# A Mamba stage in one kernel: diagonals of B through DRAM, root of token sums on GpSimd, states kept by VectorE, edges in one sum, and the pieces of a body at other slots

## The chip, the cores and the metric

The kernel runs on one core of a Trainium2 chip. A core has five engines with instruction streams of their own, each worked off in order: TensorE (PE; its weight loads are shown apart as PEld), VectorE (DVE), ScalarE (ACT), GpSimd (POOL) and SyncE (SP), which here only issues DMA transfers. They meet through semaphores. The metric is the time of one execution on the device in microseconds (us), the median of the runs; lower is better.

## The reference, cut to what matters

The whole model is a MetaFormer block: a convolution and attention layer, a recurrence over 4096 tokens (normalise, one matrix, a sigmoid), eight Mamba layers, and a mixture of experts. The change lies in the Mamba layers. For every layer, with L = 4096 tokens, four batch elements, 128 model channels, 256 inner channels d and 16 states s:

```python
xz = x @ Wi
xi, z = jnp.split(xz, 2, axis=-1)
xp = jnp.pad(xi, ((0, 0), (D_CONV - 1, 0), (0, 0)))
xc = sum((xp[:, k:k + L, :] * cw[:, k] for k in range(D_CONV))) + cb
xc = jax.nn.silu(xc)
dbl = xc @ Wx                       # 8 columns for dt, 16 for B, 16 for C
dt = jax.nn.softplus(dt_r @ Wdt + bdt)
dA = jnp.exp(dt[..., None] * A)
dBx = (dt * xc)[..., None] * Bs[:, :, None, :]
h = scan(dA, dBx)                   # h[t] = dA[t] * h[t-1] + dBx[t]
y = jnp.einsum('blds,bls->bld', h, Cs) + Dp * xc
y = y * jax.nn.silu(z)
out = rmsnorm(y @ Wo)               # x * rsqrt(mean(x * x) + eps) * w
```

## The kernel before, in words

The sequence is cut into 8 chunks of TL = 512 tokens. A *body* is one chunk of one layer of one batch element: 8 x 8 x 4 = 256 bodies, in the order chunk, layer, batch element. Channels lie on the 128 partitions, so the 256 inner channels are two halves (h = 0, 1) and tokens run along the free dimension. All data are float32.

A body has NSLOT = 16 slots. A slot is one pair of states of one half of the channels: slots 0 to 7 are half 0 with pairs 0 to 7, slots 8 to 15 half 1 with pairs 7 down to 0. In a slot j of body o the loop at the end of `mamba` issues, in this order, on whatever engine each belongs to:

- `decay` for two slots ahead: ScalarE's exponentials dA (L976), two of 128x512;
- `inputs` for one slot ahead: TensorE makes dBx, the product of dt times x with B (L998). B is a value per token, so it is brought in as a diagonal matrix: the tokens of dt times x lie on partitions (`dtxT`), and eight 64-row products with `diag` give 512 tokens x 2 states in PSUM. `diag` is built by VectorE (`diag`, L964): the transposed B (`bt`, in PSUM) times an identity, one 128x512 product per pair of states, seven a body. The last pair (slots 7 and 8) goes another way: GpSimd multiplies (`times_b`, by0 and by1, L1019), and dA lies in PSUM (dAp);
- `scan`: VectorE's two scans (L1031), hs = dA * state + dBx;
- `times_c` at every odd slot, for a group g of four states: GpSimd copies the last column of hs into `state` (L1044), and then multiplies 128x2048 values by the broadcast C (L1047), which a DMA has brought into `Cb` out of the scratch `c_d`;
- `side`, the pieces of the string `PLAN`, in two parts; between them `add_up`, TensorE's transposes that add the groups' products into yT (L1051), four slots late.

The pieces carry the rest of the body: for the next body (n) the projection (`v`), the short convolution (`tap`, VectorE; the first three tokens of a chunk need the last three of the chunk before, which `edge` computes on GpSimd, L832 to L839, and six 128x1 activations bring in, L854), silu, the gate's projection (`pz`), `pd` (dt, B and C in small), `pt` (dt in full), softplus, `dtx` (GpSimd, L937) and `turn`; for the body itself `leave`, `back`, `gate`; for the body before (q) the output projection `po` and the normalisation: `square`, `pm` (the mean over channels by a product with a matrix of 1/128, L1101), Ln and Exp on ScalarE (`log`, `rstd`), and u = pos * r on GpSimd (`u`, L1112). Where a chunk begins, the pieces s and z do a layer normalisation of the input (`mean`, `var`, `lnv`, `rstd`, `u`). Each row of `PLAN` is a slot; the letter names the body.

PSUM has two banks f0 and f1 for all pieces (`BANK` says which), four for dBx and dAp (two buffers of two), one for yT. Buffers come free when their last reader is done, and an instruction that needs one waits in its engine's stream with everything behind it. The recurrence of the layer before runs on underneath: `rec.step`, a product of 128x4 (L669) and a tanh (L672), as often in a slot as `STEPS` says; its first 576 steps run alone, and in the last 36 bodies there are none left.

ScalarE must load a table of functions where two neighbouring functions lie in different sets (ACT_TABLE_LOAD); the pieces `exp` and `ln` do that by hand.

Of the kernel before, what the change touches and what calls it, by code (L numbers as in the profile page):

```python
# [610 lines left out]
class Recurrence:  # L611
# [44 lines left out]
    def step(self, t):  # L656

        nc = self.nc
        n, k = divmod(t, RT)
        if k == 0:  # L660

            self.wx, self.x1 = self.got.pop(n)
            self.p = self.ps.tile([P, RT, B], F32, tag="p", name="p")
            nc.tensor.matmul(
                self.p, self.ops.ident, self.wx.rearrange("p b t -> p t b"), start=True, stop=False,
                skip_group_check=True,
            )
            self.z = self.w.tile([P, RT, B], F32, tag="z", name="z")
        nc.tensor.matmul(  # L669
            self.p[:, k, :], self.vt, self.before, start=False, stop=True, skip_group_check=True  # L670
        )
        nc.scalar.activation(self.z[:, k, :], self.p[:, k, :], AF.Tanh, scale=0.5)  # L672
        self.before = self.z[:, k, :]
        if k == RT // 2 and n + 1 < L // RT:
            self.load(n + 1)
        if k == RT - 1:
            y = self.w.tile([P, RT, B], F32, tag="y", name="y")
            nc.gpsimd.tensor_scalar(y, self.z, 0.5, 0.5, ALU.mult, ALU.add)
            nc.gpsimd.tensor_tensor(self.x1, self.x1, y.rearrange("p t b -> p b t"), ALU.add)
            here = (slice(None), slice(None), slice(n * RT, (n + 1) * RT))  # L680
            nc.sync.dma_start(out=self.x2_d[here], in_=self.x1)
# [11 lines left out]
s.mean n.v0 |  # L693
s.var |
| n.tap03 n.tap02 o.C3
n.v1 | q.leave1 o.by0
n.tap01 | o.by1 q.back1
q.gate1 |
| n.tap12 q.po0 n.tap13 n.tap11
q.po1 | q.square n.pz0 n.pz1 n.silu n.silu_z0 n.silu_z1 a.exp  # L700
n.pd0 | n.pd1 z.fetch n.keep
n.pt0 n.C2 n.pt1 | n.softplus0 q.pm n.softplus1 a.ln q.log q.rstd s.lnv s.rstd a.exp
n.dtx0 n.bt n.B |
q.u | s.u o.leave0 n.diag0
n.turn0 n.skip0 n.skip1 | n.diag2
o.back0 n.diag5 | q.end n.diag3
n.diag1 n.C0 o.gate0 n.dtx1 | n.C1
n.diag4 n.turn1 n.diag6 m.edge |
""".strip().split("\n")
STEPS = [1, 0, 1, 2, 1, 1, 1, 0, 1, 0, 1, 0, 2, 2, 2, 1]  # L710

BANK = {
    "v0": 0, "v1": 1, "pz0": 0, "pz1": 1, "pd": 0, "pt0": 1, "pt1": 0, "bt": 0, "turn0": 1,
    "turn1": 1, "back0": 1, "back1": 0, "po": 0, "pm": 1, "mean": 1, "var": 1,
# [12 lines left out]
def mamba(tc, ops, I, rec, x2_d, x3_d):  # L727
# [13 lines left out]
    SP_B = SP - 1  # L741
    with ExitStack() as ctx:
        dap = ctx.enter_context(tc.tile_pool(name="mda", bufs=4))
# [24 lines left out]
        i64 = c.tile([P, 64], F32, name="i64")  # L768
        nc.vector.tensor_tensor(i64, ops.ident[:, 0:64], ops.ident[:, 64:P], ALU.add)
# [10 lines left out]

        us = {}
        weights = {}
# [25 lines left out]
        def mean(o):  # L808
            m = bank("mean")
            nc.tensor.matmul(m, ops.avg, o.x2, start=True, stop=True)  # L810
            o.pos = w1.tile([P, TL], F32, tag="xm", name="xm")
            nc.vector.tensor_tensor(o.pos, o.x2, m, ALU.subtract)
            nc.scalar.activation(o.x2, o.pos, AF.Square)

        def var(o):
            o.r = w1.tile([P, TL], F32, tag="r0", name="r0")
            v = bank("var")
            nc.tensor.matmul(v, ops.avg, o.x2, start=True, stop=True)
            nc.scalar.copy(o.r, v)

        def log_var(o):
            nc.scalar.activation(o.r, o.r, AF.Ln, bias=ops.eps6)


        def edge(o):

            o.edge = w.tile([P, NH, DC - 1], F32, tag="edge", name="edge")
            part = w.tile([P, NH, DC - 1, DC - 1], F32, tag="part", name="part")
            for h in range(NH):
                tl = tail[:, o.l, o.b, h, :]  # L830
                for k in range(DC - 1):
                    nc.gpsimd.tensor_tensor(  # L832
                        part[:, h, k, :],
                        tl[:, k : k + DC - 1],
                        taps[:, o.l, h, k : k + 1].to_broadcast([P, DC - 1]),
                        ALU.mult,
                    )
            nc.gpsimd.tensor_tensor(o.edge, part[:, :, 0, :], part[:, :, 1, :], ALU.add)
            nc.gpsimd.tensor_tensor(o.edge, o.edge, part[:, :, 2, :], ALU.add)  # L839

        def proj(o, h):
# [10 lines left out]
            nc.scalar.activation(o.xc[:, h, n:], v[:, n:], AF.Copy, scale=t)  # L852
            for k in range(n):
                nc.scalar.activation(  # L854
                    o.xc[:, h, k : k + 1], v[:, k : k + 1], AF.Identity, scale=t,
                    bias=o.edge[:, h, k : k + 1],
                )
# [62 lines left out]
        def step_proj(o, h):  # L920
            if h == 0:
                o.pt = {}
            o.pt[h] = bank(f"pt{h}")
            at = W_DT + h * P
            nc.tensor.matmul(
                blocks(o.pt[h]), o.given[:, at : at + P], o.dbl, start=True, stop=True
# [31 lines left out]
        def diag(o, sp):  # L958

            if sp == 0:  # L960
                o.diag = w.tile([P, SP_B, NB, 64, 2], F32, tag="diag", name="diag")
            at = RK + 2 * sp
            bt = o.BT.rearrange("p (n r) -> p n r", n=NB)[:, :, at : at + 2]
            nc.vector.tensor_tensor(  # L964
                o.diag[:, sp],
                bt.unsqueeze(2).to_broadcast([P, NB, 64, 2]),
                i64.unsqueeze(1).unsqueeze(3).to_broadcast([P, NB, 64, 2]),
                ALU.mult,
            )


# [13 lines left out]
        def inputs(o, j):  # L985
# [8 lines left out]
            for n in range(NB):  # L994
                for q in range(2):
# [5 lines left out]
                        o.diag[row, sp, n],  # L1001
# [24 lines left out]
        def scan(o, j):  # L1026
            sp, h = where(j)
            hs = states(o, j)
            for k in range(2):
# [8 lines left out]
                )  # L1038

        def times_c(o, g):  # L1040
# [3 lines left out]
            nc.gpsimd.tensor_copy(  # L1044
                state[:, o.l, o.b, h, 4 * f : 4 * f + 4].unsqueeze(2), hs[:, :, TL - 1 : TL]
            )
# [52 lines left out]
        def rms(o):  # L1099
            o.pm = bank("pm")  # L1100
            nc.tensor.matmul(o.pm, ops.avg, o.sq, start=True, stop=True)  # L1101

        def log(o):
            o.r = w1.tile([P, TL], F32, tag="r", name="r")
            nc.scalar.activation(o.r, o.pm, AF.Ln, bias=ops.eps5)

        def rstd(o):
            nc.scalar.activation(o.r, o.r, AF.Exp, scale=-0.5)

        def norm(o):  # L1110
            o.out = us[o.b] = up.tile([P, TL], F32, tag="u", name="u")
            nc.gpsimd.tensor_tensor(o.out, o.pos, o.r, ALU.mult)  # L1112

        def end(o):
            here = (slice(None), o.b, slice(o.ck * TL, (o.ck + 1) * TL))
            x3 = w1.tile([P, TL], F32, tag="x3", name="x3")
# [13 lines left out]
        def table(name):  # L1130
# [11 lines left out]
        pieces |= {f"diag{k}": lambda o, k=k: diag(o, k) for k in range(SP_B)}  # L1142
# [3 lines left out]
            "fetch": fetch, "mean": mean, "var": var, "lnv": log_var, "silu": silu_x, "keep": keep,  # L1146
            "B": give_b,
            "bt": turn_b, "square": square, "pm": rms, "log": log, "rstd": rstd, "u": norm,
            "end": lambda o: end(o) if o.l == DEPTH - 1 else None, "edge": edge,
            "exp": table(EXP_TANH), "ln": table(EXP_LN),  # L1150
# [10 lines left out]
        for t in range(PRE):  # L1161
            rec.step(t)
        for s in bodies[0:3]:
            for what in ("fetch", "mean", "var", "lnv", "rstd", "u"):
                pieces[what](s)
        fetch(bodies[3])
        edge(bodies[0])
        for row in plan:
            for part in row:
                for k, what in part:  # L1170
                    if k == "n":
                        pieces[what](bodies[0])
        decay(bodies[0], 0)
        decay(bodies[0], 1)
        edge(bodies[1])
        inputs(bodies[0], 0)
        LAG = 4
        t = PRE
        for i in range(len(bodies) + 1):
# [3 lines left out]
            who["s"] = s if s and s.l == 0 else None  # L1183
            who["z"] = z if z and z.l == 0 else None
            if not o:
                who["a"] = None
                nc.scalar.preload_act_table_set(EXP_LN)
            if o and o.b == 1 and i + 3 < len(bodies):
                load((o.l + 1) % DEPTH)
            for j in range(NSLOT):  # L1190
                if o:
                    if j + 2 < NSLOT:
                        decay(o, j + 2)
                    elif n:
                        decay(n, j + 2 - NSLOT)
                    if j + 1 < NSLOT:
                        inputs(o, j + 1)
                    elif n:
                        inputs(n, 0)
                    if STEPS[j] > 0 and t < L:  # L1200
                        rec.step(t)
                        t += 1
                    scan(o, j)
                    if j % 2:
                        times_c(o, j // 2)
                side(who, j, 0)
                if o and j in (LAG, SP + LAG):
# [6 lines left out]
                if o and STEPS[j] > 1 and t < L:  # L1214
                    rec.step(t)
# [367 lines left out]
def layouts(a):  # L1583
# [31 lines left out]
    for h in range(NH):  # L1615
        ch = slice(h * P, (h + 1) * P)
        given[:, :, W_X + h * P : W_X + h * P + RK + 2 * NS] = f["L1_conv_W_xproj"][:, ch]
        given[:, :, W_OUT + h * P : W_OUT + (h + 1) * P] = f["L1_conv_W_out"][:, ch]
    given[:, :RK, W_DT : W_DT + DI] = f["L1_conv_W_dt"]
# [32 lines left out]
```

## Time and profile before

Three runs: median 15734.69 us (15732.74 to 15743.9). The profiled execution's own time is its span.

| | us |
|---|---|
| median of the runs | 15734.69 |
| profiled execution, span | 15742.0 |
| PE busy | 14396.9 (91%) |
| POOL busy | 13176.9 (84%) |
| DVE busy | 13692.5 (87%) |
| ACT busy | 12015.6 (76%) |
| first scan of the Mamba stage begins | 2215.23 |
| its last scans begin | 15448.80 |
| 8000 to 12000: PE, DVE, POOL, ACT busy of 4000 | 3789.45, 3682.95, 3712.28, 3207.24 |

A line of a timeline has the start and the length in us, engine, source line, operation, output<-inputs, and how many instructions it merges; in brackets, how long the engine sat idle before it and what ended that. A group of the page has busy time in all and the mean of one in ns, and after the bar the idle time before its instructions. A line of the waits says who waited for whom, in all, how often and at most. Matrix products overlap, so the distance between starts says more than their lengths.

### The profile page before, as it was taken

To read this page: it belongs to the slowest core of one execution; us is meant where nothing else is said; L and a number is where in the kernel's file an instruction comes from. 1 tells how busy PE (TensorE), PEld (TensorE's weight loads), DVE (VectorE), ACT (ScalarE), POOL (GpSimd) and SP (SyncE) were. 2 spreads that over 40 slices of the span, in tenths; PEclk is the share of its full clock that TensorE was granted. 3 is DMA by queue.
4 is the path that set the end of the run, shared out by engine and by line. 5 is a ranking of instruction groups with operands and counts; after the bars stand their busy time and mean duration, and the time that the engine had idled before them with its cause. 6 is when DMAs were issued, how large, how long until landed. Compare 5 with 4: busy or idle time off the path is not lost.

```text
span 15742.0 us, 303070 instructions
## 1 busy us (share of the span) xinstructions
PE 14396.9 (91%) x120596; PEld 10815.0 (69%) x120596; DVE 13692.5 (87%) x14955; ACT 12015.6 (76%) x23617; POOL 13176.9 (84%) x9086
## 2 busy tenths in 40 slices
PE   6888779999999999999999999999999999999996
PEld 3444557777777777777777777777777777766665
DVE  8998039998999899998999899989998999999994
ACT  6888247887888778877888788878888788777773
POOL 4555039999999999999999999999999999999994
PEclk8999569999999999999999999999999999999998
DMA  0000012222222222222222222222222222222224
GB/s 22 22 22 22 15 50 100 104 98 105 97 97 104 97 106 99 97 107 96 104 98 97 105 97 104 101 102 101 95 103 102 100 104 97 103 97 97 102 93 176
DMA packets 423478, 1431.59 MB, mean 91 GB/s; under 512 B 204080, under 2 KB 204464, under 8 KB 290864
## 3 DMA queue, kind: packets, MB, share of 16 engines
q1 hardware_dynamic: 421920, 1411.95, 24.9%
q8 instruction: 952, 15.60, 0.4%
q14 instruction: 462, 3.78, 0.1%
q10 hardware_dynamic: 144, 0.26, 0.0%
HBM read 1353.33 MB, written 58.72 MB: 90 GB/s over the span
## 4 chain that ended last, share of the span: by engine, by line
POOL 61%; issue 11%; ACT 10%; PE 9%; DVE 7%; DMA 1%; POOLq 0%; SPq 0%; ACTq 0%; DVEq 0%
POOL hs L1047 46%; POOL hs L1019 6%; POOL dtx L937 4%; ACT dA L976 4%; DVE hs L1031 2%; DVE acc L278 2%; POOL state L1044 2%; POOL u L1112 2%; PE yT L1051 2%; POOL part L832 1%; PE f L849 1%; ACT L1131 1%; PE xm L221 1%; PE dBx L998 1%; ACT xc L854 1%
## 5 line engine op out<-in xcount | busy, mean ns | idle before, releaser
L1031 DVE TENSOR_TENSOR_SCAN hs<-dA,state,dBx 128x512 f32<-128x512 f32 x7168 | 8714.0, 1262 | 992.7 <-PE dBx L998 872.1
L1047 POOL TENSOR_TENSOR hs<-hs,Cb 128x2048 f32<-128x2048 f32 x2048 | 9294.6, 4538 | 166.2 <-POOL state L1044 1.5
L976 ACT ACTIVATE dA<-dt,A 128x512 f32<-128x512 f32 x7168 | 4728.6, 722 | 7.4 <-DVE hs L1031 1.2
L1051 PE MATMUL yT<-ident,hs 128*128 128x128 f32 x32768 | 4334.5, 276 | 8.8 <-POOL hs L1047 8.8
L1051 PEld LDWEIGHTS yT<-ident,hs 128*128 128x128 f32 x32768 | 3785.6, 144 | 772.5 <-issue 650.3
L998 PE MATMUL dBx<-diag,dtxT 64*128 64x128 f32 x57344 | 4188.2, 286 | 70.9 <-DVE hs L1031 44.8
L998 PEld LDWEIGHTS dBx<-diag,dtxT 64*128 64x128 f32 x57344 | 3512.3, 188 | 1026.5 <-issue 696.9
L672 ACT ACTIVATE z<-p 128x4 f32<-128x4 f32 x4096 | 711.3, 174 | 1575.4 <-PE p L669 1569.5
L669 PE MATMUL p<-z,vt 128*128 128x4 f32 x8192 | 1579.3, 263 | 238.6 <-ACT z L672 232.4
L669 PEld LDWEIGHTS p<-z,vt 128*128 128x128 f32 x8192 | 1350.3, 207 | 635.1 <-ACT z L672 377.5
L1019 POOL TENSOR_TENSOR hs<-Bb,dtx 128x512 f32<-128x512 f32 x1024 | 1275.0, 1280 | 5.5 <-PE yT L1051 4.5
L1031 DVE TENSOR_TENSOR_SCAN hs<-dAp,state,hs 128x512 f32<-128x512 f32 x1024 | 1228.2, 1261 | 0.0
L863 DVE SCALAR_TENSOR_TENSOR xc<-f,taps,xc 128x509 f32<-128x509 f32 (+2 forms) x1536 | 1129.4, 735 | 42.2 <-ACT tail L858 15.0
L964 DVE TENSOR_TENSOR diag<-f,i 128x512 f32<-128x512 f32 x1792 | 1156.3, 669 | 9.3 <-PE f L952 9.3
L1044 POOL COPY state<-hs 128x4 f32<-128x4 f32 x2048 | 388.0, 189 | 779.9 <-DVE hs L1031 621.5
L1131 ACT ACT_TABLE_LOAD x768 | 985.3, 1283 | 10.4
L278 DVE SCALAR_TENSOR_TENSOR acc<-qp,dww,acc 128x512 f32<-128x512 f32 x1184 | 886.1, 748 | 12.2
L976 ACT ACTIVATE dAp<-dt,A 128x512 f32<-128x512 f32 x1024 | 709.1, 692 | 209.2 <-DVE hs L1031 178.1
L878 PE MATMUL f<-u,given 128*128 128x512 f32 x1024 | 510.1, 620 | 332.3 <-ACT pos L1097 322.8
L854 ACT ACTIVATE xc<-f,edge,taps 128x1 f32<-128x1 f32 x1536 | 426.6, 350 | 435.9 <-POOL edge L839 435.7
L937 POOL TENSOR_TENSOR dtx<-dt,xc 128x512 f32<-128x512 f32 x512 | 651.7, 1273 | 13.3 <-ACT dt L931 13.3
L947 ACT COPY dtxT<-f 128x512 f32<-128x512 f32 x512 | 298.0, 582 | 385.4 <-PE f L944 385.4
(237 smaller groups left out, 16083.6 us busy)
## 6 DMA issues: line engine op xcount, KB each, us to landing
Cb<-c_d SPq DMA_DIRECT2D x1024, 1024.0 KB, 4.7
Bb<-c_d SPq DMA_DIRECT2D x256, 512.0 KB, 5.5
given<-in_m_given_dram SPq DMA_DIRECT2D x64, 640.0 KB, 6.0
slab<-in_w_dram SPq DMA_DIRECT2D x60, 512.0 KB, 9.9
x<-x_d SPq DMA_DIRECT2D x96, 256.0 KB, 4.6
c_d<-dbl SPq DMA_DIRECT2D x512, 32.0 KB, 1.6
x_d<-x SPq DMA_DIRECT2D x63, 256.0 KB, 2.2
xb<-in_x_dram SPq DMA_DIRECT2D x32, 256.0 KB, 3.2
```

What stands on the lines that cost most here:

```text
L278: nc.vector.scalar_tensor_tensor(rows(to), x, dww[:, t : t + 1], rows(o.acc), ALU.mult, ALU.add)
L669: nc.tensor.matmul(self.p[:, k, :], self.vt, self.before, start=False, stop=True, skip_group_check=True)
L863: nc.vector.scalar_tensor_tensor(x, o.v[h][:, : TL - k], taps[:, o.l, h, DC - 1 - k : DC - k], x, ALU.mult, ALU.add)
L937: nc.gpsimd.tensor_tensor(to, blocks(o.dt[h]), blocks(o.xc[:, h, :]), ALU.mult)
L964: nc.vector.tensor_tensor(o.diag[:, sp], bt.unsqueeze(2).to_broadcast([P, NB, 64, 2]), i64.unsqueeze(1).unsqueeze(3).to_broadcast([P, NB, ...
L976: nc.scalar.activation(o.dA[j][:, k, :], o.dt[h], AF.Exp, scale=A[:, o.l, h, n : n + 1])
L998: nc.tensor.matmul(o.dBx[j][:, at : at + 64, :], o.dtxT[h][row, n, :], o.diag[row, sp, n], start=True, stop=True,)
L1019: nc.gpsimd.tensor_tensor(hs[:, k, :].rearrange("p (q n t) -> p q n t", n=NB, q=2), o.Bb[:, k, :].rearrange("p (q n t) -> p q n t", n=NB, ...
L1031: nc.vector.tensor_tensor_scan(hs[:, k, :], o.dA[j][:, k, :], hs[:, k, :] if sp == SP_B else o.dBx[j][:, :, k], state[:, o.l, o.b, h, s : ...
L1047: nc.gpsimd.tensor_tensor(hs, hs, o.Cb[f], ALU.mult)
L1051: nc.tensor.matmul(o.yT[:, n, :], x[:, n * P : (n + 1) * P], ops.ident, start=start and n == 0, stop=True, is_transpose=True, skip_group_c ...
L1131: return lambda o: nc.scalar.preload_act_table_set(name)
```

## The change

- **Diagonals.** The zeros of `diag` are written once: three spare blocks in DRAM are filled with zeros at the start. `spread` then copies 14 values of B per token out of the transposed B (ScalarE, `bts`) and writes them by two DMAs onto the diagonals of a spare block, in pieces of 14 values; `diag` loads the whole block (128 x 3584 values, 1.835 MB) by one DMA. VectorE's seven products are gone.
- **Root.** The mean over channels is taken with the tokens on partitions: `sums` makes four products of one column each, `inverse` adds eps on VectorE and raises to the power -0.5 on GpSimd (128x4), `rows` spreads the result again by four transposes into PSUM, and VectorE makes u. Ln and Exp on ScalarE go, and GpSimd's u. The same for the layer normalisation of the input.
- **States.** `hold`, on VectorE, copies the last column of a finished group into `state`, behind the first scan of the next slot; `times_c` comes one slot later.
- **Edges.** One product of 128x18 on GpSimd instead of six; the sum is added by VectorE once (`edges`) instead of by six activations.
- **dt.** `pt` is done on rows 0 to 63 for half 0 and 64 to 127 for half 1; the weights are laid out for it.
- **Order.** `PLAN`, `STEPS` and `BANK` are new, `rec.step` is split from its tanh, dA has five buffers for four, and `turn1` moves into the body itself.

```diff
 PLAN = """
...
+s.mean m.edge n.v0 | s.var
+o.turn1 s.rv | n.tap02
+o.C3 n.v1 | n.tap01
+n.tap03 | o.C2 n.edges q.leave1
+o.by0 | q.back1
+| q.gate1 n.tap12
+n.tap13 n.tap11 q.po0 q.po1 |
+q.square q.pm | a.exp q.rstd q.ru q.u o.by1 n.silu n.pz0 n.silu_z0 n.pz1 n.silu_z1
+n.pd0 q.end | n.pd1 n.keep s.rr
+z.fetch | n.bt n.B s.first
+n.spread n.pt0 n.pt1 | n.softplus0 n.softplus1
+| o.leave0 n.dtx0
+n.C1 n.dtx1 a.exp | n.diag n.turn0
+| n.skip0
+| o.back0 n.skip1
+| n.C0 o.gate0
...
-STEPS = [1, 0, 1, 2, 1, 1, 1, 0, 1, 0, 1, 0, 2, 2, 2, 1]
+STEPS = [2, 1, 1, 2, 1, 2, 1, 2, 0, 0, 0, 1, 1, 1, 1, 0]
...
-        dap = ctx.enter_context(tc.tile_pool(name="mda", bufs=4))
+        dap = ctx.enter_context(tc.tile_pool(name="mda", bufs=5))
...
+        zero = w.tile([P, NB, 64, ND], F32, tag="diag", name="zero")
+        nc.gpsimd.memset(zero, 0.0)
+        spares = [dr.tile([P, NB, 64, ND], F32, tag=f"spare{k}", name="spare", bufs=1) for k in range(3)]
+        for spare in spares:
+            nc.sync.dma_start(out=spare, in_=zero)
...
+        def sums(o, of, what):
+
+            o.ms = bank(what)
+            for n in range(NB):
+                nc.tensor.matmul(
+                    o.ms[:, n : n + 1], of[:, n * P : (n + 1) * P], ops.avg[:, 0:1],
+                    start=n == 0, stop=True, skip_group_check=True,
+                )
+
+        def inverse(o, eps):
+
+            o.r = w.tile([P, NB], F32, tag="r", name="r")
+            nc.vector.tensor_scalar(o.r, o.ms[:, 0:NB], eps, None, ALU.add)
+            nc.gpsimd.tensor_tensor(o.r, o.r, power, ALU.pow)
+
+        def rows(o, what):
+
+            o.R = bank(what)
+            for n in range(NB):
+                nc.tensor.transpose(
+                    o.R[:, n * P : (n + 1) * P], o.r[:, n : n + 1].to_broadcast([P, P]), ops.ident
+                )
...
+        def add_edge(o):
+
+            x = o.xc[:, :, 0 : DC - 1]
+            nc.vector.tensor_tensor(x, x, o.edge, ALU.add)
...
-                blocks(o.pt[h]), o.given[:, at : at + P], o.dbl, start=True, stop=True
+                blocks(o.pt[h]), o.given[rows, at : at + P], o.dbl[rows], start=True, stop=True
...
+        def spread(o):
+
+            small = w.tile([P, NB, ND], F32, tag="bts", name="bts")
+            nc.scalar.copy(small, o.BT.rearrange("p (n r) -> p n r", n=NB)[:, :, RK : RK + ND])
+            o.spare = spares[bodies.index(o) % len(spares)]
+            for q in range(2):
+                half = o.spare[q * 64 : (q + 1) * 64]
+                line = half.ap[0][0]
+                to = bass.AP(half.tensor, half.offset, [[line + ND, 64], [64 * ND, NB], [1, ND]])
+                nc.sync.dma_start(out=to, in_=small[q * 64 : (q + 1) * 64])
+
+        def diag(o):
+
+            o.diag = w.tile([P, NB, 64, ND], F32, tag="diag", name="diag")
+            nc.sync.dma_start(out=o.diag, in_=o.spare)
...
+                if k == 0:
+                    while ended:
+                        hold(*ended.pop())
+            if j % 2:
+                ended.append((o, j // 2))
+
+        def hold(o, g):
+            sp, h = where(2 * g)
+            f = sp // 2
+            nc.vector.tensor_copy(
+                state[:, o.l, o.b, h, 4 * f : 4 * f + 4].unsqueeze(2), o.hs[g][:, :, TL - 1 : TL]
+            )
...
-            nc.gpsimd.tensor_copy(
-                state[:, o.l, o.b, h, 4 * f : 4 * f + 4].unsqueeze(2), hs[:, :, TL - 1 : TL]
-            )
             nc.gpsimd.tensor_tensor(hs, hs, o.Cb[f], ALU.mult)
...
         def norm(o):
             o.out = us[o.b] = up.tile([P, TL], F32, tag="u", name="u")
-            nc.gpsimd.tensor_tensor(o.out, o.pos, o.r, ALU.mult)
+            nc.vector.tensor_tensor(o.out, o.pos, o.R, ALU.mult)
...
                     scan(o, j)
-                    if j % 2:
-                        times_c(o, j // 2)
+                    if j % 2 == 0 and j:
+                        times_c(o, j // 2 - 1)
```

## The prediction

> **What bounds the kernel now.** I read the page first (busy times and costliest groups), then the timeline of single engines over one body, then the chain of waits. Page:
>
> ```profile
> span 15742.0 us, 303070 instructions
> PE 14396.9 (91%) x120596; PEld 10815.0 (69%) x120596; DVE 13692.5 (87%) x14955; ACT 12015.6 (76%) x23617; POOL 13176.9 (84%) x9086
> ...
> L1031 DVE TENSOR_TENSOR_SCAN hs<-dA,state,dBx 128x512 f32<-128x512 f32 x7168 | 8714.0, 1262 | 992.7 <-PE dBx L998 872.1
> L1047 POOL TENSOR_TENSOR hs<-hs,Cb 128x2048 f32<-128x2048 f32 x2048 | 9294.6, 4538 | 166.2 <-POOL state L1044 1.5
> L964 DVE TENSOR_TENSOR diag<-f,i 128x512 f32<-128x512 f32 x1792 | 1156.3, 669 | 9.3 <-PE f L952 9.3
> L1044 POOL COPY state<-hs 128x4 f32<-128x4 f32 x2048 | 388.0, 189 | 779.9 <-DVE hs L1031 621.5
> ```
>
> PE, DVE and POOL are all nearly full, so no share names the bound. It is read in one body (256 in all, 16 slots each). VectorE's timeline, start and length in us:
>
> ```profile
> 9000.10 2.44 DVE L1031 TENSOR_TENSOR_SCAN hs<-dA,state,dBx 128x512 f32<-128x512 f32 x2
> ...
> 9022.91 2.29 DVE L863 SCALAR_TENSOR_TENSOR xc<-f,taps,xc 128x510 f32<-128x510 f32 x3
> 9025.11 4.80 DVE L1031 TENSOR_TENSOR_SCAN hs<-dAp,state,hs 128x512 f32<-128x512 f32 x4
> 9029.83 2.43 DVE L1031 TENSOR_TENSOR_SCAN hs<-dA,state,dBx 128x512 f32<-128x512 f32 x2
> 9033.00 2.45 DVE L1031 TENSOR_TENSOR_SCAN hs<-dA,state,dBx 128x512 f32<-128x512 f32 x2 [0.75 <-PE dBx L998]
> 9038.03 2.45 DVE L1031 TENSOR_TENSOR_SCAN hs<-dA,state,dBx 128x512 f32<-128x512 f32 x2 [2.58 <-PE dBx L998]
> ...
> 9051.05 2.44 DVE L1031 TENSOR_TENSOR_SCAN hs<-dA,state,dBx 128x512 f32<-128x512 f32 x2
> ```
>
> The period is 9051.05-9000.10 = 50.95. VectorE idles 0.75+2.58 = 3.33 in it, both times for dBx. TensorE's timeline ahead of the second stall:
>
> ```profile
> 9025.58 1.98 PE L878 MATMUL f<-u,given 128*128 128x512 f32 x4 [1.21 <-ACT pos L1097]
> 9027.62 1.16 PE L998 MATMUL dBx<-diag,dtxT 64*128 64x128 f32 x16
> 9028.96 1.10 PE L892 MATMUL f<-xc,given 128*128 128x512 f32 x2
> 9029.90 1.04 PE L1051 MATMUL yT<-ident,hs 128*128 128x128 f32 x8
> 9031.73 1.16 PE L998 MATMUL dBx<-diag,dtxT 64*128 64x128 f32 x16
> 9032.82 1.98 PE L925 MATMUL f<-dbl,given 128*128 128x512 f32 x4
> 9035.70 1.12 PE L1101 MATMUL f<-sq,avg 128*128 128x512 f32 x2
> 9036.76 1.16 PE L998 MATMUL dBx<-diag,dtxT 64*128 64x128 f32 x16
> ```
>
> TensorE waits for `pos`, then works without a gap for 12.3 us. So the loop is: VectorE without a gap from scan 11 to scan 6 of the next body (12 slots x 2.36, seven diagonals x 0.59, two gates x 0.59, three taps 2.06 = 35.7), ScalarE's dAp, sq and pos (2.7), TensorE (12.4), crossings 0.1: 50.9, as measured. Chain of waits from 4000 to 12000:
>
> ```profile
> DVE hs L1031 <- PE dBx L998: 527.1, 319, 3.0
> PE f L878 <- ACT pos L1097: 186.0, 154, 1.2
> ```
>
> That is 3.4 and 1.2 us a body. TensorE is close behind: by distances between starts, 14 dBx x 1.09, 16 yT x 1.02, eleven 512-column products x 0.94, seven groups of four transposes x 0.48, 16 steps x 0.24 = 49.1.
>
> [...] 16 64-row passes take 1.09 (0.07 each), transposes of the same 128 columns over all rows 0.12 each. [...] c_d (32 KB) lands in 1.6 us, Cb (1 MB) in 4.7; the last stage moves 418 GB/s.
>
> **The change part by part, per body.**
>
> VectorE: -7 diagonals x 0.59 = -4.1; +0.59 for u (like a gate); +8 state copies, +1 edge sum, +1 addition of eps, each 0.13-0.16 (RECIPROCAL 128x4: 0.167): +1.4. Net -2.1.
>
> GpSimd: -8 state copies x 0.27, -u 1.25, -five small edge instructions 0.9; +one power. Net about -3.9.
>
> ScalarE: -Ln, Exp 1.3, -six edge activations 1.7, +bts 0.2, +1.28, since the new program's order has six table loads for five. It is 80% busy; its burst ends before TensorE needs it (gate0 over 1 us ahead of pd0).
>
> TensorE: -pm 0.94, + four one-column products like steps 0.96, + four transposes 0.48; dt's products on two 64-row tiles: one of four passes overlaps, -0.47 (between 0 and -0.94). Net 0: 49.1 remains the floor.
>
> SP: +2 spread writes (256 pieces of 56 B each), +1 diag load (1.835 MB). New order: c_d x2, Bb, spread x2, C1, diag, C0, C3, C2. C1 waits for times_c of group 4 of the body ahead, and diag stands behind it. Landing, as an estimate: 2.1 + 2.88 MB/418 GB/s = 9 us after times_c 4. Counting from the copy of group 4 (in slot 10): 0.1+4.5+0.1+9 = 13.7. TensorE comes to the next body's first dBx 14.2 after that copy (in the loop below, 8.9 and 23.1 after its start), and VectorE needs the product 0.5 later than it would be ready: hidden, with 0.5 to 1 us to spare; beyond that each us late costs one. The spread itself lands some 2 us after bts, while C1 still waits. Behind a late diag on TensorE stand all later dBx and yT; behind diag on SP only C0, C3 and C2, which are needed a third of a body later.
>
> The new loop. VectorE from scan 14 to scan 7 of the next body: ten slots 23.6, two gates 1.2, six taps 4.0, edge sum 0.16, five copies 0.65: 29.6. Then serially: eps 0.16, crossing 0.1, power, crossing 0.1. Then TensorE from the rows of the root to dBx 14: transposes 0.48, pz 1.9, six dBx 6.5, pd 1.9, five yT 5.1, bt, xD and dtxT 1.45, dt 1.4, two steps 0.5 = 19.25; crossing 0.1. Power: no row shows one; from below 0.19 (any small GpSimd instruction), from above some 2; I take 0.4.
> The copy of group 2 meets times_b: GpSimd does times_c 1 and by0 in 4.5+2.5 = 7.0 after copy 1, VectorE arrives after 6.0. [...] +1.05; queued behind it on VectorE are the rest of scan 6, two taps, scan 7 and the addition of eps, for which GpSimd's power and TensorE's rows wait. The other seven copies come, in this ledger, when GpSimd has just finished (least room: 0.05 at group 3, after by1), and the edge sum 0.3 after times_c 0: they cost nothing[...]. Without the lock the power waits 0.3 for times_c 2 instead. Sum: 29.6+1.05+0.76+19.25+0.1 = 50.8.
>
> Edits at nothing: the split of step and tanh, the fifth dA buffer and C2 and C3 given in the body itself lie under ScalarE's and SP's slack (Cb lands in 4.7, its use is over 8 us off); turn1, moved into slot 1 of its own body, is needed at slot 9; the zeros and three first writes of the spare blocks lie under the recurrence's start (400 us in which GpSimd waits). If that slack were gone, turn1 would cost its 0.5 and copy 0.6 once.
>
> So the freed 3.33 of stalls come back elsewhere: scans 10, 12 and 14 wait for dBx, and VectorE waits for u. 50.8 against 50.95 is -0.13. Over some 190 ordinary bodies: -25 us. The last 36 (period 51.5 at clock 0.97, no steps; now about 50.6): -32. Where a chunk of the sequence begins (seven times, up to 60.7 us for a body; 3.07 us of it TensorE at `var` waiting for the square), the sums are shorter and u leaves GpSimd: -6 each, -40 (0 to -100). Start-up with the diagonal's three transfers: +10. Sum -87 from 15742.0: 15655. The median of runs, 15734.7, is 7 lower: **15650**.
>
> **Rivals.**
> *Copies don't wait* [...]: 50.0 a body, -0.93x190-1.7x36-40+10 = -268: 15470. TensorE's 49.1 allows it. [...]
> *The power is slow*: it stands alone on the loop with VectorE and TensorE both waiting. From 0.75 us the gain is gone; at 2 us, +1.6x256 = 410: 16060. For: nothing in the trace prices it. This is the case on the other side.
> *diag lands late*: if 56 B pieces or the load run slower (the 1.4 MB mask took 7.0 at the start: 284 GB/s after 2 us; so 12 us): 2 us late, 16050. For: 36 GB/s more on a queue that SP serves in order. Against: 418 GB/s shown.
> *Nothing comes of it*: TensorE's load doesn't fall, so small waits fill the rest: within 0.2%.
>
> **How the numbers follow.** Likeliest 0.40 (own range 15560-15740; a ledger of the old body came out within 0.1 us, but the new one has three unknown terms), copies free 0.25, slow power 0.20 (from 0.75 to beyond 2 us), late diag 0.13, nothing 0.02. Faster: 0.30 of the likeliest and 0.24 of free copies; slower: 0.04 of the likeliest, 0.19 of the slow power, 0.12 of the late diag; the rest lies within 0.2%. Measurement tells about 0.2% (31 us). Faster 0.54, same 0.11, slower 0.35. The range reaches from just below the second case to short of 2 us for the power: 15400 to 16000.
>
> **What would show it.** Right: a period near 50.8; diag group gone; VectorE idle ahead of u for PE, then ahead of scans 10, 12, 14; state copies whose mean is far above 0.16, ending with a GpSimd instruction; small waits for diag. Wrong: copies at 0.16 throughout; a power row over 0.75 us; dBx waiting for the DMA of diag; dt's products still 1.8 us for two.

## The result, and the profile after

The changed kernel takes 16150.56 us (median of 4 runs, 16122.52 to 16196.4), the kernel before, beside it, 15733.72 us. The ratio is 1.0267, 95% interval 1.0247 to 1.0287: slower by 417 us, where 15650 was forecast. The profiled execution took 16177.3 us; its mean granted TensorE clock is 0.938, against 0.964 before.

The page of the changed kernel, with the rows that answer to those shown of before (the last row is a DMA with its time to landing):

```profile
span 16175.5 us, 306984 instructions
...
PE 14668.7 (91%) x123476; PEld 11191.0 (69%) x123476; DVE 13541.4 (84%) x16043; ACT 11646.9 (72%) x21977; POOL 12634.0 (78%) x5759
...
PEclk8999579999999999999999999999999999999998
...
L1086 POOL TENSOR_TENSOR hs<-hs,Cb 128x2048 f32<-128x2048 f32 x2048 | 9290.5, 4536 | 1750.0 <-DVE state L1078 1064.8
L1061 DVE TENSOR_TENSOR_SCAN hs<-dA,state,dBx 128x512 f32<-128x512 f32 x7168 | 8833.9, 1265 | 1001.3 <-PE dBx L1028 965.5
...
L1028 PE MATMUL dBx<-diag,dtxT 64*128 64x128 f32 x57344 | 4235.1, 285 | 368.0 <-DMA diag<-spare 293.5
...
L1078 DVE COPY state<-hs 128x4 f32<-128x4 f32 x2048 | 793.4, 387 | 0.0
...
diag<-spare SPq DMA_DIRECT2D x256, 1792.0 KB, 9.5
```

VectorE and GpSimd have less work than before, and TensorE is busy for 272 us longer. Two rows stand out: the state copies take 387 ns each, where the smallest take 131, and TensorE waits 293.5 us for the diagonal's DMA.

VectorE's timeline around the root in one body:

```profile
9082.72 1.27 DVE L1061 TENSOR_TENSOR_SCAN hs<-dA,state,dBx 128x512 f32<-128x512 f32 x1
9083.91 0.78 DVE L1078 COPY state<-hs 128x4 f32<-128x4 f32 x1
9084.60 1.27 DVE L1061 TENSOR_TENSOR_SCAN hs<-dA,state,dBx 128x512 f32<-128x512 f32 x1
9085.79 1.50 DVE L890 SCALAR_TENSOR_TENSOR xc<-f,taps,xc 128x509 f32<-128x509 f32 x2
9087.21 2.45 DVE L1061 TENSOR_TENSOR_SCAN hs<-dAp,state,hs 128x512 f32<-128x512 f32 x2
9089.57 0.14 DVE L841 TENSOR_SCALAR r<-f 128x4 f32<-128x4 f32 x1
9091.91 0.69 DVE L1140 TENSOR_TENSOR u<-pos,f 128x512 f32<-128x512 f32 x1 [2.20 <-PE f L848]
```

The copy of group 2 takes 0.78 us: it ends when GpSimd's two `times_b` (9082.16 to 9084.66) end. So it is with all 740 copies that took more than 250 ns: each ends 22 to 34 ns behind the end of an instruction of GpSimd (the lock, below). Then, as forecast, VectorE stands still for u (2.20), while GpSimd raises to the power and TensorE spreads the result. TensorE in the same stretch, and below it windows of 2 us; there the granted clock is the last column but two (after start:end, length and busy time):

```profile
9087.95 1.05 PE L833 MATMUL f<-avg,sq 128*128 128x1 f32 x8 [0.91 <-ACT sq L1134]
9088.86 0.36 PE L669 MATMUL p<-z,vt 128*128 128x4 f32 x2
9089.09 1.07 PE L1090 MATMUL yT<-ident,hs 128*128 128x128 f32 x8
9090.86 0.94 PE L848 MATMUL f<-ident,r 128*128 128x128 f32 x4 [0.69 <-POOL r L842]
9091.59 3.32 PE L905 MATMUL f<-u,given 128*128 128x512 f32 x4
```

```profile
9088.00:9090.00 2.00, 2.00 (x18) 1.00 0.00 0
9090.00:9092.00 2.00, 1.30 (x7) 0.77 0.00 0
9092.00:9094.00 2.00, 2.00 (x3) 0.50 0.00 0
```

The two z projections take 3.32 us, with 0.50 granted from 9092 to 9094; in the kernel before the same two took 1.98 (at 9025.58), with 1.00 granted. In the trace the half clock comes in stretches of 3.41 us or multiples of it, on a fixed grid. Between the first gate and the last there are 42 such stretches before (177 us) and 261 after (1089 us); 208 of the 261 begin at the root, 53 in the first 4 us after gate 0, where the first dBx waits for diag. The 42 bodies without such a stretch last 51.85 us in the mean, all bodies 53.43; before, all bodies took 51.70 in the mean.

The waits from 4000 to 12000, after:

```profile
DVE hs L1061 <- PE dBx L1028: 543.6, 765, 3.0
DVE u L1140 <- PE f L848: 322.6, 139, 3.0
PE dBx L1028 <- DMA diag<-spare: 166.0, 125, 3.1
```

Some 150 bodies lie in this window, so the three waits are 3.6, 2.2 and 1.1 us in each.

### The profile page after: what moved, and what is told of

It is laid out like the page before. It is cut to its first block, busy times and chain, and to the rows that moved or that the text cites. A ratio compares the mean times of both kernels' runs of the same rounds, so it can differ in the third digit from the quotient of the medians.

```text
span 16175.5 us, 306984 instructions
## 1 busy us (share of the span) xinstructions
PE 14668.7 (91%) x123476; PEld 11191.0 (69%) x123476; DVE 13541.4 (84%) x16043; ACT 11646.9 (72%) x21977; POOL 12634.0 (78%) x5759
## 5 line engine op out<-in xcount | busy, mean ns | idle before, releaser
L1061 DVE TENSOR_TENSOR_SCAN hs<-dA,state,dBx 128x512 f32<-128x512 f32 x7168 | 8833.9, 1265 | 1001.3 <-PE dBx L1028 965.5
L1028 PE MATMUL dBx<-diag,dtxT 64*128 64x128 f32 x57344 | 4235.1, 285 | 368.0 <-DMA diag<-spare 293.5
L1090 PE MATMUL yT<-ident,hs 128*128 128x128 f32 x32768 | 4462.6, 280 | 3.7 <-POOL hs L1086 3.7
L1090 PEld LDWEIGHTS yT<-ident,hs 128*128 128x128 f32 x32768 | 3835.9, 148 | 707.0 <-issue 616.5
L1061 DVE TENSOR_TENSOR_SCAN hs<-dAp,state,hs 128x512 f32<-128x512 f32 x1024 | 1272.6, 1271 | 2.0 <-POOL hs L1049 2.0
L890 DVE SCALAR_TENSOR_TENSOR xc<-f,taps,xc 128x510 f32<-128x510 f32 (+2 forms) x1536 | 1117.1, 727 | 16.1 <-ACT tail L885 2.9
L1078 DVE COPY state<-hs 128x4 f32<-128x4 f32 x2048 | 793.4, 387 | 0.0
L905 PE MATMUL f<-u,given 128*128 128x512 f32 x1024 | 716.2, 831 | 4.7 <-DVE xc L890 4.1
L884 ACT ACTIVATE xc<-f,taps 128x512 f32<-128x512 f32 x512 | 352.3, 688 | 489.1 <-PE f L881 345.7
L1140 DVE TENSOR_TENSOR u<-pos,f 128x512 f32<-128x512 f32 x256 | 176.1, 688 | 615.0 <-PE f L848 572.8
```

Source lines behind the costliest of these rows:

```text
L890: nc.vector.scalar_tensor_tensor(x, o.v[h][:, : TL - k], taps[:, o.l, h, DC - 1 - k : DC - k], x, ALU.mult, ALU.add)
L905: nc.tensor.matmul(o.pz[h], o.given[:, at : at + P], o.u, start=True, stop=True)
L1028: nc.tensor.matmul(o.dBx[j][:, at : at + 64, :], o.dtxT[h][row, n, :], o.diag[row, n, :, 2 * sp : 2 * sp + 2], start=True, stop=True,)
L1061: nc.vector.tensor_tensor_scan(hs[:, k, :], o.dA[j][:, k, :], hs[:, k, :] if sp == SP_B else o.dBx[j][:, :, k], state[:, o.l, o.b, h, s : ...
L1078: nc.vector.tensor_copy(state[:, o.l, o.b, h, 4 * f : 4 * f + 4].unsqueeze(2), o.hs[g][:, :, TL - 1 : TL])
L1090: nc.tensor.matmul(o.yT[:, n, :], x[:, n * P : (n + 1) * P], ops.ident, start=start and n == 0, stop=True, is_transpose=True, skip_group_c ...
```

## The experiments

There are four suspects: the clock, the late diagonal, the locked copies and the slow power. Each was first taken away alone from the changed kernel. A result gives the median of four runs, its ratio to the kernel before with the 95% interval, and the distance from the changed kernel's 16150.56 us; by the two intervals, such a distance is uncertain by some 40 us.

**1. 128 columns instead of one.**

```diff
-  o.ms[:, n : n + 1], of[:, n * P : (n + 1) * P], ops.avg[:, 0:1],
-  start=n == 0, stop=True, skip_group_check=True,
+  o.ms[:, n * P : (n + 1) * P], of[:, n * P : (n + 1) * P], ops.avg,
+  start=True, stop=True,
...
-  o.r, o.ms[:, 0:NB], eps, None, ALU.add
+  o.r, o.ms.rearrange("p (n c) -> p n c", n=NB)[:, :, 0], eps, None, ALU.add
```

> The four one-column products that sum a token's squares stream 128 columns each instead of 1 (same stationary blocks, same sums, written 128 times side by side); nothing else changes. Theory A (the half clock comes from stretches in which TensorE streams few columns, and one-column products count as idle): of the 261 half-clock intervals in the recurrence some 200 lie at the root and go; mean granted clock back from 0.938 to about 0.96; the sums take the same 0.95 us; 1.2 to 1.6 us a body, 15750 to 15850 us. Rival B (only true gaps of TensorE count, these are unchanged): clock stays at 0.94, time within 30 us of 16150. Rival C (the loss is the power and the late diagonal, the clock is a bystander): clock may rise, time stays above 16050.

15979.64 us, ratio 1.0157 (1.0140 to 1.0174): 171 us less. The clock is 0.963, and 20 half-clock stretches begin at the root instead of 208. TensorE and its clock at the root:

```profile
9044.74 1.16 PE L833 MATMUL f<-avg,sq 128*128 128x128 f32 x8 [0.91 <-ACT sq L1134]
9045.73 0.28 PE L669 MATMUL p<-z,vt 128*128 128x4 f32 x2
9045.88 1.07 PE L1090 MATMUL yT<-ident,hs 128*128 128x128 f32 x8
9047.65 0.65 PE L848 MATMUL f<-ident,r 128*128 128x128 f32 x4 [0.70 <-POOL r L842]
9048.14 2.14 PE L905 MATMUL f<-u,given 128*128 128x512 f32 x4
```

```profile
9046.00:9048.00 2.00, 1.30 (x12) 1.00 0.01 4
9048.00:9050.00 2.00, 2.00 (x7) 1.00 0.00 0
```

The idle times are the same as above, 0.91 and 0.70; only the columns that pass through the array between them are more, and the clock stays at 1.00. So it was not the gaps alone (rival B falls), and the clock costs time (rival C falls). The gain is about half of what was expected: TensorE's waits for diag rise from 294 to 360 us, so part of the time won at the root is waited away at the next first dBx.

**2. The diagonal's load one slot earlier on SyncE's queue.**

```diff
-| o.leave0 n.dtx0
-n.C1 n.dtx1 a.exp | n.diag n.turn0
+| o.leave0 n.dtx0 n.diag
+n.C1 n.dtx1 a.exp | n.turn0
```

> Only the load of the diagonal is moved, one slot earlier on SyncE's queue, ahead of C1, which waits for a product by C. Theory A with late diagonal as second cause: TensorE's waits for diag, 293 us in all, go to under 50; the 53 half-clock intervals after the body's first dBx go, those at the root stay; clock about 0.945; 100 to 300 us less, 15850 to 16050. Rival (the wait for diag is hidden, or the load waits for the write of the spread blocks itself): waits stay over 200 us or time within 40 us of 16150.

16010.77 us, 1.0174 (1.0158 to 1.0189): 140 us less. The wait for diag falls from 293.5 to 21.3 us. In the changed kernel the queue stands at C1 until GpSimd is done with a group; the load follows, and its transfer runs together with C1's megabyte. In the body shown a second wait comes on top: the load reads what the two spread writes have written, the later of them lands at 9052.31, and the load goes out at 9052.38:

```profile
9047.03 1.24 SPq L995 DMA_DIRECT2D spare<-bts  x2
9049.60 0.33 SPq L943 DMA_DIRECT2D Cb<-c_d  x1
9052.38 0.33 SPq L1000 DMA_DIRECT2D diag<-spare  x1
```

The later spread write of a body takes 3.1 us to land (median), the first 3.5, and 95 of the 256 loads go out within 0.2 us of such a landing: they waited for it, and no longer for C1. From C1's issue to diag's landing the median is 10.2 us. Ahead of C1, the load waits for the spread writes alone, and takes 7.5 us from issue to landing instead of 9.5:

```profile
diag<-spare SPq DMA_DIRECT2D x256, 1792.0 KB, 7.5
```

The expectation for the time and the waits was met, that for the clock was not: of the half-clock stretches at the first dBx one is left, but those at the root grow to 236, many of twice the length, and the clock is 0.935, not 0.945.

**3. The copies as a maximum over one element.**

```diff
-  nc.vector.tensor_copy(
-      state[:, o.l, o.b, h, 4 * f : 4 * f + 4].unsqueeze(2), o.hs[g][:, :, TL - 1 : TL]
+  nc.vector.tensor_reduce(
+      state[:, o.l, o.b, h, 4 * f : 4 * f + 4], o.hs[g][:, :, TL - 1 : TL], AX.X, ALU.max
```

> The eight state copies on VectorE are written as a maximum over an inner axis of one element: same data, same place in the order[...]. Theory L (the copies' mean of 387 ns is the lock with GpSimd): mean 140 to 180 ns, VectorE's busy time 450 to 500 us less; time 0 to 250 us less, since part of the lock lay under other waits. Rival (the copies wait for something else, such as the scan's write): mean stays near 390 ns and time within 40 us of 16150.

16012.22 us, 1.0177 (1.0162 to 1.0192): 138 us less. The copies' row:

```profile
L1078 DVE TENSOR_REDUCE state<-hs 128x4 f32<-128x4 f32 x2048 | 275.4, 134 | 0.0
```

As theory L said, 387 ns have become 134, so 518 us of VectorE's time were waiting, 2.0 us a body. The place in the order, the data and the semaphores are the same; the form of the instruction decides. Why it does, no run shows.

**4. A product in place of the power.** `ALU.pow` becomes `ALU.mult` on GpSimd.

> GpSimd multiplies by -0.5 where the changed kernel raises to the power -0.5, so the root is left out of the computation; all waits and the order stay. The row falls from 1.02 to about 0.2 us. Theory P (my step: the power is serial on the loop): 0.8 us a body and fewer half-clock intervals at the root: 200 to 350 us less, 15800 to 15950. Rival A (the clock is lost to the low activity of the sums and the wait for the square, which stay): 50 to 150 us less at most, clock under 0.95. Rival H (hidden): within 40 us of 16150.

15972.33 us, 1.0152 (1.0137 to 1.0167): 178 us less, between the two expectations. The power's row in the changed kernel:

```profile
L842 POOL TENSOR_TENSOR r<-r,power 128x4 f32<-128x4 f32 x288 | 291.3, 1011 | 147.4 <-DVE r L841 147.4
```

The product takes 203 ns in this run. The clock is 0.945; 144 half-clock stretches begin at the root instead of 208.

**5, 9, 10, 11. The three edits that keep the computation, together and in pairs.**

> The edits of the 128-column sums, the earlier load of the diagonal and the copies written as a maximum, together. If the three are separate costs (theory A): their single gains, 171+140+138 = 449 us, add up: 15700, between 15660 and 15760, clock above 0.97. If they are one loop's slack seen three times (rival: TensorE's order, with its waits for the square and the power, bounds what is left): 15800 to 15900, with those two waits as large as before or larger.

15453.62 us, 0.9819 (0.9804 to 0.9833) of before: 697 us less than the changed kernel, where the single gains add up to 449, and 1.8% faster than the kernel before. It is better than both expectations: the gains do more than add up. Two gates of the same kind, one body apart, in VectorE's timeline:

```profile
9030.87 0.67 DVE L1122 TENSOR_TENSOR y<-f,gate 128x512 f32<-128x512 f32 x1
...
9080.64 0.67 DVE L1122 TENSOR_TENSOR y<-f,gate 128x512 f32<-128x512 f32 x1
```

A body takes 49.77 us (every fourth takes 51.6), and the clock is 0.967. Then each edit was left out of the three:

> The three edits without the 128-column sums: earlier load of the diagonal and copies as a maximum, one-column sums as in the changed kernel. Theory S (TensorE at half clock behind the root becomes the bound once nothing else holds the loop): the clock falls to about 0.935 again, some 250 intervals at half clock, and the time rises from 15454 by more than the 171 us that the wide sums won alone: 15700 to 15850. Rival (each edit has its own fixed price): 15625.

15673.29 us, 0.9957 (0.9943 to 0.9972): 220 us more than with all three. The clock (0.94) and the 231 half-clock stretches are close to what theory S said; the time lies between the two expectations, 48 us above the fixed price and 27 below the range of theory S.

> The three edits without the earlier load: the diagonal's load stands behind C1 again. Theory S: TensorE's waits for diag of 0.8 to 1.4 us a body are back in full, since a shorter body leaves the load less time: 15650 to 15850. Rival (fixed price): 15594. Rival H (with VectorE and GpSimd no longer locked, C1's wait ends earlier and so does the load's): waits for diag under 0.4 us a body, 15460 to 15550.

15832.23 us, 1.0058 (1.0043 to 1.0073): 379 us more, where the edit alone had won 140. TensorE waits 1.39 us a body for diag again (355 us in all); theory S holds, and rival H falls.

> The three edits without the maximum: the state copies are plain copies again. Theory L: copies' mean back to 0.30 to 0.40 us, of which more lies on the loop than the 138 us won alone: 15600 to 15800. My prediction's loop has one lock of 1.05 us a body: 15454+270 = 15720. Rival (fixed price): 15592.

15651.02 us, 0.9942 (0.9926 to 0.9959): 197 us more. This is in theory L's range, and below the 270 us of the prediction's one lock. The copies take 364 ns, 1.8 us a body more than as maxima, of which 0.8 is seen in the time.

All eight combinations are now measured. The gain of each edit, averaged over the six orders in which the three can be made, is 220 us for the wide sums, 284 for the early load, 193 for the copies. The early load is worth 140 us alone, 329 with the wide sums in place, 339 with the maxima, 379 with both; the wide sums 171 alone and 360 with the load early. Without the early load, wide sums and maxima just add up (171 and 138 alone, 318 together); with it they bring 360 and 337 alone and 557 together. So the late diagonal hides 239 us of the other two: of what they save, TensorE waits a part away for a DMA whose start hangs on GpSimd and SyncE (294 us of waits in the changed kernel, 355 with the other two edits made).

**12. The power, with the three edits in.**

> The three edits, and GpSimd multiplies where it raises to the power, so the root is left out of the computation. Theory P (the power is serial on the loop, and the loop runs through VectorE, the root and TensorE, as in my prediction): 0.8 us a body less, 15200 to 15300. Rival (TensorE's own 49.1 us bounds a body of 49.8): at most 0.3 us a body, 15370 to 15450.

15294.30 us, 0.9717 (0.9702 to 0.9731): 159 us less than with the power; an ordinary body takes 49.3. The time lies at the edge of theory P's range, but the price is not the whole one: of 0.81 us taken off the loop 0.5 is gained in an ordinary body, 0.62 in the mean. When the short product ends, TensorE is often not free yet: from there to the rows of the root the median is 0.40 us where it was 0.06, since the eight transposes of the states stand ahead of them.

**6 and 7. TensorE's order.**

```diff
-q.square q.pm | a.exp q.rstd q.ru q.u o.by1 n.silu n.pz0 n.silu_z0 n.pz1 n.silu_z1
+q.square | q.pm a.exp q.rstd n.pz0 q.ru q.u o.by1 n.silu n.silu_z0 n.pz1 n.silu_z1
```

> One row of the plan: the sums of the squares stand behind eight transposes of the states, and the first z projection of the next body stands between the sums and the transposes of the root. No instruction is added or removed. Theory G (the loss is TensorE held at the head of its queue, first for the square, then for the power): both waits, 1.2 and 0.55 us a body, go to under 0.4 in all; half-clock intervals at the root go with them; 300 to 450 us less, 15700 to 15850. Rival D (VectorE's wait for u sets the loop, and the root's chain is as long as before, or longer by the projection): within 60 us of 16150, or slower.

16156.97 us, 1.0262 (1.0245 to 1.0279): no change. The waits for the square and the power fall from 1.21 and 0.57 to 0.23 and 0.07 us a body, and TensorE waits 0.31 for VectorE's addition of eps and 0.85 for u instead, since the second z projection needs the bank that u still reads. VectorE's wait for u is 2.18 (2.24). Rival D holds: moved about inside the root's chain, TensorE's gaps are worth nothing. The half-clock stretches fall from 261 to some 145 (1089 to some 830 us), so half clock doesn't cost its length everywhere either.

> The three edits and the new order of TensorE together. Theory A with G: TensorE has no wait over 0.3 us a body left, 49.1 to 50.0 a body, 15350 to 15550. Rival (VectorE's chain bounds it: scan 14 to scan 7, root, rows): 15650 to 15750.

15541.74 us, 0.9877 (0.9862 to 0.9892): 88 us slower than the three edits without it. That is in the range of theory A, but by the three edits, not by the order. The sums now stand behind eight transposes of the states and begin 0.7 us behind the square (0.05 without the new order), so VectorE's addition of eps waits 132.5 us for them, where it waited 19.5; from the power to the rows nothing has changed (0.06 us).

**8. The copies back on GpSimd.**

> The state copies go back to GpSimd, ahead of the product by C, as in the kernel before; all else as in the changed kernel. Theory L: VectorE loses the lock and the copies, 3.1 us a body, GpSimd gains 2.2 of work that it has room for (78% busy): 100 to 250 us less, 15900 to 16050, like the copies written as a maximum. Rival (GpSimd's power and products start later behind the copies, which then delay the root): 16100 to 16250.

16559.82 us, 1.0524 (1.0508 to 1.0540): both expectations missed, 409 us slower. The sum of the edges on VectorE (6 values from two SBUF tiles) took 0.15 us; here its row is

```profile
L871 DVE TENSOR_TENSOR xc<-xc,edge 128x6 f32<-128x6 f32 x256 | 967.0, 3777 | 0.0
```

This is 3.8 us each. In 251 of 256 bodies the sum ends 18 to 26 ns behind the end of a `times_c` of 4.5 us, into which it now falls; GpSimd in turn waits 682 us (147) for VectorE's addition of eps. Why the two wait for each other, no run shows.

## Why the prediction was wrong, point by point

The direction was wrong: the forecast was 500 us too low. The loop was right in form. What put it on the other side is one size, the power, one term taken as nothing, the wait for diag, and one that is missing, the clock; the two other errors, the lock and dt's products, went the other way. As an estimate from these runs, in us of the whole: power +159 (0.62 a body), diag +284 and clock +220 (averages over the orders), lock -76 (193 for 269), dt -120 (0.47 a body). That makes 467 of the 500; the rest is open.

**The new loop** (VectorE from scan 14 to scan 7, the root, TensorE to dBx 14, 50.8 us). With the lock taken out (-1.05), the power at its measured 1.02 (+0.62) and dt's products as measured (below, -0.47 more) it is 49.9; the run with the three edits has 49.77. There the parts can be read one by one:

```profile
9038.52 0.16 DVE L841 TENSOR_SCALAR r<-f 128x4 f32<-128x4 f32 x1
...
9058.65 1.28 DVE L1061 TENSOR_TENSOR_SCAN hs<-dA,state,dBx 128x512 f32<-128x512 f32 x1 [0.72 <-PE dBx L1028]
...
9088.29 0.16 DVE L841 TENSOR_SCALAR r<-f 128x4 f32<-128x4 f32 x1
```

From scan 14 to the addition of eps there are 29.6 us (29.6 forecast), from there to the rows of the root (at 9039.83, one body earlier) 1.3, and from the rows to scan 14 18.8, where 19.25 less 0.47 and a crossing make 18.9. In us of the whole, 15650 with these corrections, 256 bodies each, is 15420; measured are 15454.

**Power, 0.4 us: mis-sized.** The 0.4 was a guess between a measured 0.19 and a guessed 2, since no row of before has a power. It takes 1.01 to 1.02. The rival named it, with a threshold of 0.75 above which the gain is gone. It costs 178 us alone and 159 with the others gone.

**The lock, 1.05 us at group 2 alone: found, but elsewhere and cheaper.** That the copy would wait for GpSimd was the author's assumption; the trace of before has no such wait to show it. The copies wait 2.0 us a body, of which group 2 has 0.53. The ledger gave the other copies hardly any room (0.05 at group 3) and called that nothing; in the trace the copies of groups 2, 5, 6 and 7 take 0.67, 0.54, 0.93 and 0.38 us in the mean, the others 0.14 to 0.16. In the time it is worth 193 us in the average over the orders, less than the 269 that the 1.05 stood for: this error did not make the forecast too low.

**diag, "hidden, with 0.5 to 1 us to spare": the step that failed most.** From the copy of group 4 on, the prediction reckoned 13.7 us to diag's landing and 14.2 to TensorE's arrival; the medians are 15.0 and 13.8. So the landing comes 10.2 us after `times_c` 4 and not 9, and TensorE is there 0.4 sooner. The estimate had the bytes of both transfers in it; its 2.1 us ahead of them is near what `Cb` of before leaves, 4.7 us for 1.05 MB, less 2.5 at 418 GB/s. What it lacked is that diag's own issue comes after C1's, by 0.74 us in the mean and 2.8 in the body shown, and that the spread writes, put at 2 us, take 3.1 and 3.5 and were what the load waited for last in 95 bodies. TensorE waits 1.1 us a body for diag in the profile, in 202 bodies; by the times of landing, the first dBx starts 0.14 us behind the diagonal in 250 of 256. It is worth 284 us in the average. The rival was there, with a chance of 0.13.

**The clock: not in the prediction.** In the page the clock's digits are 9 through the whole stage, after (above) and before alike, so the loss shows only in its mean (0.964 before, 0.938 after) and in short windows:

```profile
PEclk8999569999999999999999999999999999999998
```

The sums counted a product as a product: four one-column products at 0.96 us stand in for one of 512 columns at 0.94. In time they are alike, but hardly any columns pass through the array in them. It is worth 220 us in the average.

**dt's products on row tiles, -0.47: too little.** That one of four passes overlaps was the author's estimate. The two took 1.02 us from first to last where they took 1.98, which is at the lower bound (-0.94) that the step named.

**Signs as forecast.** Seen were copies far above 0.16 that end with GpSimd, VectorE idle ahead of u, and waits ahead of scans 10, 12 and 14. Of the signs that would speak against, two were seen: dBx waiting for the diagonal's DMA, and a power row over 0.75 us. A period near 50.8 was not seen; it is 53.4.

## What to carry to other kernels

Sources of lateness can hide one another: taken away one by one the three gave 449 us here, together 697, and it was the late DMA that hid the others. So try the pairs before you call an edit worthless. When a product is swapped for another of the same length, compare the columns it streams as well (with one column the mean clock was 0.938 here, with 128 columns 0.963), and look at the granted clock behind every place where TensorE has gaps. A small copy is not small if it has to wait for a long instruction on another engine: here a change of its form took the wait away (387 to 134 ns), and a change of its engine moved the wait to another instruction (0.15 to 3.8 us).

## What the runs showed of the hardware

- In the traces of both kernels the half clock goes with how little streams through the array. Count 0.94 ns a column as streaming (four transposes of 128 columns took 0.48 us), and half of it for a 64-row pass (16 of them, of 128 columns each, took 1.09 us), and sort the grid intervals of 3.41 us that were at full clock. In the changed kernel, of 231 with under 40% of streaming all were followed by one at half clock, of 53 with 40 to 45% 31, of 3389 above that none; in the kernel before 41 of 41, 2 of 9 and none of 3762. In experiments 6 and 8 there are exceptions, 45 of 3586 and 11 of 3468 intervals above 45%. By TensorE's busy time the intervals do not part: of those that were 60 to 75% busy, 157 of 290 were followed by half clock in the changed kernel, and none of 234 before. At the root shown, gaps of 0.91 and 0.69 us with one-column products between them were followed by a granted 0.50; gaps of 0.91 and 0.70 us with 128 columns in their place left it at 1.00.
- GpSimd's power on 128x4 values takes 1.01 us, a product on the same values 0.20.
- VectorE's maximum over an inner axis of one element copies 128x4 values in 134 ns beside a busy GpSimd; a plain copy took up to 1.8 us there.
- A table load on ScalarE took 1.28 us. In the body of before from 9000 to 9051 there are five, ahead of silu, dA, softplus, Ln and dA; between dA and the recurrence's tanh there is none.
